# An attention stage with interleaved pieces: the last slot of each step left empty, a wide silu(c), and idle products in bare slots

## The chip, the cores and the metric

The kernel runs on one core of one Trainium2 chip. The time is the device time of one execution in microseconds. Of the kernel before there are three runs: 1338.03, 1338.38 and 1339.69 us, median 1338.38. One more execution was profiled.

## The reference

One transformer block with adaptive layer norm on 8 rows of 512 tokens of width 256 (4096 tokens), all in float32:

```python
mod = (_silu(c) @ wmod).reshape(8, 6, 1, -1)           # c: 8 x 256, wmod: 256 x 1536
sa, ca, ga, sb, cb, gb = (mod[:, k] for k in range(6)) # gates ga, gb: sign kept, size at least 0.25
h = _layernorm(x) * (1 + ca) + sa
x = x + ga * attention(h)     # 16 heads of 16, latent of 64, causal, softmax in full
h = _layernorm(x) * (1 + cb) + sb
x = x + gb * ffn(h)           # 16 experts, each takes its 512 best tokens, and a shared expert
```

In the attention, query and key of a head are `q_lat` (through `q_to_latent`) and `latent_k`, the value is `latent_v`, and `v_up` and `Wout` follow. For the change it matters that the causal logits of a head (512 x 512) are needed twice: once to find each row's maximum, and once, transposed and with the maximum taken off, to be exponentiated and multiplied with the values. Silu(c) is a matrix of 8 x 256 that is multiplied with `wmod` once.

## The kernel before

The kernel has two stages of engine work that follow each other: the attention stage, to about 515 us of the span, and the experts. The change touches only the first.

**Start.** Layer-norm statistics, `sc` = silu(c) transposed (two chunks `k` of 128 partitions x 8, lines 203 to 206), and the products of `sc` with the modulation weights: `pmT` (line 215) gives shift and scale for the first norm; `modulate(n)` (line 227) gives gates and second shift and scale with the 8 columns of `sc` as the stationary operand and 512 columns of weights streaming (`pm`); `modulate_t` (line 234) gives shift and scale of the second norm transposed, with the weights stationary and the 8 columns of `sc` streaming (`pmT2`). `keep_warm` products (line 182) stand at the very start.

**Steps.** Row b and head group g (4 heads) make step n = 4b + g, 32 steps in all. The main loop runs n from -1 to 31. In turn n it works on three steps at once: the contexts (attention times values) of step n-1, `context`, line 678, tile `po`; the transposed scores and exponentials of step n (`scores_t`, tile `st_ps`, and `exps`, line 652); and the plain scores and maxima of step n+1 (`scores`, tile `sc_ps`, and `maxima`, line 627). Contexts stand first, then `fold` (line 640): four transposes of the maxima into `pmx`, and a DVE subtraction from the query strip. After that come six half rounds `k`. A half round takes two heads of the plain scores and two heads of the transposed scores, on different row strips of the array, so that they run side by side, for the tiles that `ROUNDS` names. Within a half round PE gets plain, transposed, plain, transposed; then DVE gets the maxima of the two heads, and ScalarE the two exponentials, with POOL's causal selects behind them.

Plain scores lie in a ring of three PSUM banks (`bank_s`), transposed ones in another (`bank_t`); step -1, which has no transposed scores, uses both. Other products share two banks (`bank`, tag `m`).

**Pieces.** All other products of the attention stage are cut into pieces of about 0.44 us and put between the half rounds: queries (`pq`) and keys (`pk`) of step n+2, transposes (`pt`) and latents (`pl`) of the next row, values (`pv`, line 511), the residual (`py`, line 544), the second norm's transposes and router scores (`pz`, `pzt`), and the shared expert's gate, up and down products (`pg`, `pu`, `py`, lines 303 to 348). `plan(n)` lists a step's pieces, each with an earliest slot, an estimate in us, and DVE work that it brings. There are seven slots: slot 0 ahead of half round 0, and so on to slot 6 behind half round 5, ahead of the next step's contexts. `laid_out` (line 842) places the pieces. It runs a small model of PE and DVE with the constants `ROUND_US`, `HEAD_US`, `CHANGE_US` and `FOLD_US`, gets from it the PE time that each slot should hold (`need`), spreads what is left evenly over the slots, and goes through the pieces in order: each goes into the current slot, or further on if that slot's share is used up. A piece with estimate 0 goes to the slot that the plan names.

Each engine runs its instructions in the order in which this loop issues them. The value piece has a wait of its own: `value(i2, iis)` writes two products into the halves of one PSUM bank, and ScalarE copies each half out after its product:

```python
if ii == 0:
    self.pv = bank("pv").rearrange("p (i h w) -> p i h w", h=H, w=DH)
...
nc.scalar.copy(v[:, i, :, 0:HS:2], self.pv[:, ii, :, :])
```

The second product of a bank waits for the copy of the first. Gate pieces end with a tanh on ScalarE and a DVE product, up pieces with a DVE product (`mid`), residual pieces with a DVE addition. `query` and `key` end with a ScalarE copy and two DMA issues on the SP queue (`spread`, line 581), which bring the rows into the query and key strips.

Of the kernel before, what the change touches and what calls it, by code (L numbers as in the profile page):

```python
# [12 lines left out]
F32 = mybir.dt.float32  # L13
# [8 lines left out]
P = 128  # L22
B, T, D = 8, 512, 256
# [5 lines left out]
KC = D // P  # L29
# [22 lines left out]
def block_kernel(ctx: ExitStack, tc: tile.TileContext, a: dict, out: bass.AP):  # L52
    nc = tc.nc
# [42 lines left out]
    sbT = const.tile([P, KC, B], F32, name="sbT")  # L96
    cbT = const.tile([P, KC, B], F32, name="cbT")
# [18 lines left out]
    ap = att.enter_context(tc.tile_pool(name="att", bufs=2))  # L116
# [13 lines left out]
    wq = wp.tile([P, KC, H * DH], F32, name="wq")  # L130
# [4 lines left out]
    wmod1 = fp.tile([P, 2, KC, 512], F32, name="wmod1", tag="mid")  # L135
# [67 lines left out]
    sc = wp.tile([P, KC, B], F32, name="sc")  # L203
    nc.scalar.activation(sc, cT, AF.Tanh, scale=0.5)
    nc.vector.scalar_tensor_tensor(sc, sc, 1.0, cT, ALU.add, ALU.mult)
    nc.vector.tensor_scalar_mul(sc, sc, 0.5)

    nc.vector.tensor_reduce(strip_one, ident[:, 1::HS], AX.X, ALU.add)

    for t in k_strips:  # L210
        nc.vector.tensor_copy(t, strip_one.to_broadcast([P, T]))
    pmT = bank("pmT")[:, 0 : 2 * KC * B].rearrange("p (m b) -> p m b", b=B)
    for m in range(2 * KC):
        for k in range(KC):
# [11 lines left out]
    mod_sb = wp.tile([B, 4 * D], F32, name="mod_sb")  # L226

    def modulate(n):
        pm = bank("pm")[0:B, :]
        for k in range(KC):  # L230
            nc.tensor.matmul(pm, lhsT=sc[:, k, :], rhs=wmod1[:, n, k, :], start=(k == 0), stop=(k == KC - 1))
        nc.vector.tensor_copy(mod_sb[:, n * 512 : (n + 1) * 512], pm)

    def modulate_t():

        pmT = bank("pmT2")[:, 0 : 2 * KC * B].rearrange("p (m b) -> p m b", b=B)
        for m in range(2 * KC):
            n, c = divmod(m, KC)
            o = (1 - n) * D + c * P
            for k in range(KC):  # L240
                nc.tensor.matmul(
                    pmT[:, m, :],
                    lhsT=wmod1[:, n, k, o : o + P],
                    rhs=sc[:, k, :],
                    start=(k == 0),
                    stop=(k == KC - 1),
                )
        nc.vector.tensor_copy(sbT, pmT[:, 0:KC, :])
        nc.vector.tensor_scalar_add(cbT, pmT[:, KC : 2 * KC, :], 1.0)

    def gate(o):

# [490 lines left out]
    SLOTS = 2 * len(ROUNDS) + 1  # L743

    def plan(n):
# [93 lines left out]
    ROUND_US = (1.04, 1.04, 0.83, 0.83, 0.84, 0.84)  # L839
    HEAD_US = (0.72, 0.72, 0.6, 0.6, 0.78, 0.78)  # L840

    def laid_out(todo):

        slots = [[] for _ in range(SLOTS)]
        extra, given = [0.0] * SLOTS, [0.0] * SLOTS
        for s, us, dve, fn in todo:
            if us == 0.0:
                slots[s].append(fn)
                extra[s] += max(0.0, dve)
                given[s] += max(0.0, -dve)  # L850
        total = sum(us for _, us, _, _ in todo)
        need = [0.0] * SLOTS
        pe = BEGIN_US
        dve = ready = pe + FOLD_US
        for k in range(SLOTS):
            pe += given[k] + (CHANGE_US if k > 0 else 0.0)
            need[k] = max(0.0, ready - pe)
            pe += need[k]
            dve = max(dve + extra[k], pe)
            if k < SLOTS - 1:  # L860
                pe += ROUND_US[k]
                dve = max(dve, pe)
                ready = dve + HEAD_US[k]
                dve += 2 * HEAD_US[k]
        share = min(1.0, total / sum(need))
        rest = max(0.0, total - sum(need)) / SLOTS
        room = [share * sum(need[: k + 1]) + rest * (k + 1) for k in range(SLOTS)]
        done, floor = 0.0, 0
        for s, us, dve, fn in todo:
            if us > 0.0:  # L870
                floor = max(floor, s)
                while floor < SLOTS - 1 and done + us / 2 > room[floor]:
                    floor += 1
                slots[floor].append(fn)
                done += us
        return slots

# [7 lines left out]
    for k in range(2):  # L885
        modulate(k)
# [8 lines left out]
    for n in range(-1, len(steps)):  # L895
        last = steps[n - 1] if n > 0 else None
        now = steps[n] if n >= 0 else None
        nxt = steps[n + 1] if n + 1 < len(steps) else None
        slots = laid_out(plan(n))

        def fill(k):
            for fn in slots[k]:
                fn()

        if last is not None:
            last.context(list(range(TT)))
        if now is not None:
            now.fold()
        fill(0)
        for k in range(2 * len(ROUNDS)):  # L910
            (tiles, cs), half = ROUNDS[k // 2], k % 2

            sc_of, st_of = {}, {}
            at_s = at_t = 0
            for part, (i, c) in enumerate(zip(tiles, cs)):
                for jj in range(2):
                    if nxt is not None:
                        j = 2 * (1 - half) + jj
                        if part == 0:
                            sc_of[j] = bank_t("sc_ps") if nxt.n == 0 and j % 2 else bank_s("sc_ps")  # L920
                        nxt.scores(sc_of[j], j, i, at_s)
                    if now is not None:
                        j = 2 * half + jj
                        if part == 0:
                            st_of[j] = bank_t("st_ps")
                        now.scores_t(st_of[j], j, c, at_t)
                at_s += (i + 1) * P
                at_t += T - c * P
            for jj in range(2):
                if nxt is not None:  # L930
                    j, at = 2 * (1 - half) + jj, at_s

                    for i in reversed(tiles):
# [76 lines left out]
    with tc.tile_pool(name="srch", bufs=2) as sp, tc.tile_pool(name="srch1", bufs=1) as s1:  # L1010
# [22 lines left out]
        for bit in range(29, -1, -1):  # L1033
            part = sp.tile([P, 1], F32, name="part")
# [29 lines left out]
        one = s1.tile([P, 1], F32, name="one")  # L1064
# [27 lines left out]
    with ExitStack() as s:  # L1092
# [219 lines left out]
        for e in range(E):  # L1312
            w, t = weights.pop(e), fetches[e]
# [119 lines left out]
```

## Time and profile before

| what | us |
|---|---|
| runs, median of 3 | 1338.38 (1338.03 to 1339.69) |
| the profiled execution | 1339.74 |
| its span, first to last instruction | 1338.0 |
| TensorE busy in the span | 1306.6 |
| VectorE (DVE) busy | 897.3 |
| GpSimd (POOL) busy | 542.4 |
| ScalarE (ACT) busy | 466.6 |
| mean granted TensorE clock | 0.988 |

Busy time counts the stretches in which an engine has at least one instruction open; for PE, several products can be open side by side. A float32 product of 256 columns shows as two records, x2. In a timeline the columns are start, duration, engine, line, operation, tile written and tiles read, tile shape, operand shape and count; idle time ahead of the group and what ended it stand in brackets. In a table of stretches each engine has its busy time and, in parentheses, its number of instructions; behind them come the granted clock of TensorE as a share of full speed, the busy share of the DMA engines and GB/s.

The fold of each step marks where it begins. Lengths from fold to fold, in us:

| step | from | length |
|---|---|---|
| 0 | 35.40 | 17.06 |
| 1 | 52.45 | 12.34 |
| 3 | 80.32 | 11.36 |
| 6 | 123.06 | 16.54 |
| 8 | 153.39 | 15.42 |
| 13 | 229.78 | 16.36 |
| 14 | 246.14 | 15.43 |
| 24 | 401.56 | 15.96 |
| 28 | 463.56 | 17.82 |

### The profile page before, as it was taken

The page shows a single profiled execution, that of the slowest core. Times are in us where ns is not written, and L with a number is a line of the kernel's source. Part 1 is how long each engine was busy: PE and PEld are TensorE (multiplying, and loading weights), DVE is VectorE, ACT ScalarE, POOL GpSimd, SP SyncE. Part 2 cuts the span into 40 slices and gives each one's busy share as a digit, 9 for nine tenths or more (in the row PEclk, how much of TensorE's full clock was granted, in tenths as well). Part 3 has the DMA queues.
Part 4 walks back from the last instruction along what each step waited for, and adds up shares of the span by engine and source line. Part 5 has one row for each costly group of instructions (what it writes and reads, how often), then busy time and mean ns, then how long its engine had stood idle before and what let it go on. Part 6 is the DMA issues. An engine that isn't in the chain of part 4 may idle for free. (4 is left out here: it accounts for less than half of the span.)

```text
span 1338.0 us, 26423 instructions
## 1 busy us (share of the span) xinstructions
PE 1306.6 (98%) x10286; PEld 929.1 (69%) x10286; DVE 897.3 (67%) x2342; ACT 466.6 (35%) x997; POOL 542.4 (41%) x629
## 2 busy tenths in 40 slices
PE   9999999999999999999999999999999999999996
PEld 5344445445545455877857888888888888888885
DVE  4777676776676765566835777667777677777653
ACT  1455555555555545200112233222233222233221
POOL 4453625253544324010024455534555544555431
PEclk8899999999999999999999999999999999999998
DMA  7112322131313232271024444454444554443511
GB/s 221 60 52 58 86 46 79 40 74 47 85 38 73 57 66 53 38 238 40 21 73 118 114 135 100 128 139 119 110 137 94 138 135 122 108 138 86 145 17 16
DMA packets 84317, 121.93 MB, mean 91 GB/s; under 512 B 14936, under 2 KB 61656, under 8 KB 84192
## 3 DMA queue, kind: packets, MB, share of 16 engines
q1 hardware_dynamic: 69120, 93.76, 23.3%
q0 software_dynamic: 14336, 25.70, 10.2%
q8 instruction: 81, 1.33, 0.4%
q10 hardware_dynamic: 736, 0.79, 0.2%
q14 instruction: 44, 0.36, 0.1%
HBM read 90.33 MB, written 21.51 MB: 84 GB/s over the span
## 5 line engine op out<-in xcount | busy, mean ns | idle before, releaser
L630 DVE CUSTOM_DVE_ANT_0 sc_ps<-sc_ps,causal 128x256 f32<-128x256 f32 (+3 forms) x512 | 245.0, 510 | 89.2 <-PE st_ps L567 73.6
L1261 PE MATMUL epy<-dw,emid 128*128 128x256 f32 x1024 | 236.0, 382 | 1.4 <-ACT xT L1161 0.4
L1286 POOL DMA_INDIRECT out<-eo,idx x64 | 102.0, 1594 | 315.7 <-DVE eo L1278 191.0
L663 ACT ACTIVATE p<-st_ps 128x384 f32<-128x384 f32 (+1 forms) x384 | 181.2, 523 | 137.6 <-PE st_ps L567 135.3
L669 POOL TENSOR_SCALAR_AFFINE_SELECT p<-p 128x256 f32<-128x256 f32 x256 | 104.0, 419 | 286.6 <-ACT p L663 286.5
L1261 PEld LDWEIGHTS epy<-dw,emid 128*128 128x128 f32 x1024 | 192.0, 190 | 37.9 <-DVE emid L1231 12.4
L567 PE MATMUL sc_ps<-k,q 32*64 32x256 f32 (+3 forms) x2048 | 212.8, 458 | 3.6 <-DVE mx L630 3.5
L567 PE MATMUL st_ps<-q,k 32*64 32x128 f32 (+3 forms) x2048 | 209.2, 452 | 0.0
L1208 ACT COPY c<-eu 128x256 f32<-128x256 f32 x120 | 44.7, 373 | 400.3 <-issue 222.8
L1191 PE MATMUL eu<-xsum,wsum 128*128 128x256 f32 x720 | 176.1, 381 | 0.0
L1191 PEld LDWEIGHTS eu<-xsum,wsum 128*128 128x128 f32 x720 | 135.7, 190 | 17.9
L1191 PE MATMUL eu<-xT,gu 128*128 128x256 f32 x480 | 142.8, 379 | 0.0
L567 PEld LDWEIGHTS sc_ps<-k,q 32*64 32x64 f32 x2048 | 78.1, 132 | 79.2 <-issue 39.4
L1210 DVE TENSOR_TENSOR c<-eu,c 128x256 f32<-128x256 f32 x120 | 51.0, 425 | 100.8 <-ACT c L1209 95.5
L1148 POOL DMA_INDIRECT rows<-rows_d,idx x64 | 62.3, 974 | 137.6 <-DVE mid L327 96.4
L1231 DVE SCALAR_TENSOR_TENSOR emid<-eu,ub,esg 128x512 f32<-128x512 f32 x128 | 90.1, 743 | 28.9 <-ACT esg L1227 19.4
L1227 ACT ACTIVATE esg<-eu,gbias 128x512 f32<-128x512 f32 x128 | 81.5, 684 | 58.0 <-PE eu L1191 33.3
L1191 PEld LDWEIGHTS eu<-xT,gu 128*128 128x128 f32 x480 | 91.2, 190 | 12.4
L1211 DVE TENSOR_TENSOR eu<-eu,c 128x512 f32<-128x512 f32 x120 | 83.9, 699 | 4.1
L567 PEld LDWEIGHTS st_ps<-q,k 32*64 32x64 f32 x2048 | 76.8, 131 | 11.1 <-ACT p L663 4.0
L684 PE MATMUL po<-p,v 128*32 128x512 f32 (+3 forms) x1024 | 79.4, 444 | 0.2 <-POOL p L669 0.2
L1108 DVE TENSOR_TENSOR at_q<-pos_lo,iota 128x1024 bf16<-128x1024 f32 x64 | 75.2, 1217 | 0.0
(187 smaller groups left out, 1963.3 us busy)
## 6 DMA issues: line engine op xcount, KB each, us to landing
gu<-in_gw SPq DMA_DIRECT2D x16, 1024.0 KB
gu<-in_up SPq DMA_DIRECT2D x16, 1024.0 KB
dw<-in_dw SPq DMA_DIRECT2D x16, 1024.0 KB
q<-q SPq DMA_DIRECT2D x32, 128.0 KB
rows_d<-mod_d SPq DMA_DIRECT2D x8, 512.0 KB
rows_d<-row SPq DMA_DIRECT2D x8, 512.0 KB
out<-ysb SPq DMA_DIRECT2D x16, 256.0 KB
k<-k SPq DMA_DIRECT2D x30, 128.0 KB
```

The costliest lines, as they stand in the source:

```text
L567: nc.tensor.matmul(out[w : w + P // 2, :], lhsT=lhsT[:, w : w + P // 2], rhs=rhs, start=True, stop=True)
L630: nc.vector.tensor_tensor_reduce(sc_ps[:, at : at + n], sc_ps[:, at : at + n], causal[:, T - n : T], 1.0, -3.0e38, ALU.add, ALU.max, self. ...
L663: nc.scalar.activation(self.all[:, j, :], st_ps[:, 0:n], AF.Exp, scale=SCALE)
L669: nc.gpsimd.affine_select(out=p, in_=p, pattern=[[0, 2], [1, P]], compare_op=ALU.is_ge, fill=0.0, base=0, channel_multiplier=-1,)
L684: nc.tensor.matmul(self.po[self.strip(j), c * P : T], lhsT=v[:, c, self.g * NG + j, :], rhs=self.p[c][:, j, :], start=(c == 0), stop=(c == ...
L1108: nc.vector.tensor_tensor(self.at_q[:, n, :], pos_lo[:, e, n].unsqueeze(2).to_broadcast([P, QT, P]), iota.unsqueeze(1).to_broadcast([P, QT ...
L1191: nc.tensor.matmul(self.u[:, q, :], lhsT=w, rhs=x, start=start, stop=True, skip_group_check=not start)
L1211: nc.vector.tensor_tensor(u[:, 1:3, :], u[:, 1:3, :], c3.unsqueeze(1).to_broadcast([P, 2, HC]), ALU.add)
L1227: nc.scalar.activation(sg, pg, AF.Silu, bias=gbias[:, e, f : f + 1])
L1231: nc.vector.scalar_tensor_tensor(mid[:, f, :], pu, ub[:, e, f : f + 1], sg, ALU.add, ALU.mult)
L1261: nc.tensor.matmul(self.py[:, jj, :], lhsT=self.mid[:, f, j * P : (j + 1) * P], rhs=self.dw[:, f, :], start=(n == 0), stop=(n == NF - 1),)
L1286: nc.gpsimd.indirect_dma_start(out=out[:, :], out_offset=bass.IndirectOffsetOnAxis(ap=t.idx[:, j : j + 1], axis=0), in_=eo[:, jj, :], in_o ...
```

## The change

Four edits are made.

1. `sc_wide` repeats silu(c) sixteen times along the free axis (128 columns per chunk instead of 8), by one POOL instruction. `modulate` takes all 128 columns as the stationary operand and copies out the first 8 rows; `modulate_t` streams 64 columns and copies out the first 8. `pmT` stays as it is.
2. `laid_out` puts no sized piece into slot 6. What is left over is spread over six slots, and the contexts of the next turn follow half round 5 directly. Pieces with estimate 0 that the plan names for slot 6 stay there.
3. `laid_out` notes the load of each slot. In the turns up to n = 5, a half round whose slot holds no sized piece begins with an idle product: a full-array product of 256 columns, written into the first plain-score bank and overwritten by the scores. By the built program there are 3 of them in turn -1, 3 in turn 0, 6 in each of turns 1 and 3, and 1 in turn 4.
4. In half round 0, the plain scores of both heads stand ahead of the transposed ones.

In the built program the pieces of step 8, by slot (0 to 6), stand like this; `pv` is a value, the number is how many:

```
before  pq 3 | pq 1 | pk pv | pk pv | pv | pv pu | pu 3
after   pq 3 | pq 1 | pk pv pk pv | pv 2 | pu 1 | pu 3 | -
```

Steps 12, 16 and 20 are alike. Step 24 has `pv 2` in one slot in both. Step 28 goes from `pk pv | pv 2 pg` to `pk pv 3`.

```diff
+    sc_wide = ap.tile([P, T], F32, name="sc_wide", tag="one", bufs=1)[:, 0 : KC * P]
+    sc_wide = sc_wide.rearrange("p (k r b) -> p k r b", k=KC, b=B)
+    nc.gpsimd.tensor_scalar_mul(sc_wide, sc.unsqueeze(2).to_broadcast([P, KC, P // B, B]), 1.0)
...
     def modulate(n):
-        pm = bank("pm")[0:B, :]
+        pm = bank("pm")
         for k in range(KC):
-            nc.tensor.matmul(pm, lhsT=sc[:, k, :], rhs=wmod1[:, n, k, :], start=(k == 0), stop=(k == KC - 1))
-        nc.vector.tensor_copy(mod_sb[:, n * 512 : (n + 1) * 512], pm)
+            nc.tensor.matmul(
+                pm,
+                lhsT=sc_wide[:, k].rearrange("p r b -> p (r b)"),
...
+        nc.vector.tensor_copy(mod_sb[:, n * 512 : (n + 1) * 512], pm[0:B, :])
...
                     lhsT=wmod1[:, n, k, o : o + P],
-                    rhs=sc[:, k, :],
+                    rhs=sc_wide[:, k, 0 : P // 2 // B, :].rearrange("p r b -> p (r b)"),
...
-            need[k] = max(0.0, ready - pe)
+
+            need[k] = max(0.0, ready - pe) if k < SLOTS - 1 else 0.0
...
-        rest = max(0.0, total - sum(need)) / SLOTS
-        room = [share * sum(need[: k + 1]) + rest * (k + 1) for k in range(SLOTS)]
+        rest = max(0.0, total - sum(need)) / (SLOTS - 1)
+        room = [share * sum(need[: k + 1]) + rest * min(k + 1, SLOTS - 1) for k in range(SLOTS)]
...
-                while floor < SLOTS - 1 and done + us / 2 > room[floor]:
+                while floor < SLOTS - 2 and done + us / 2 > room[floor]:
                     floor += 1
                 slots[floor].append(fn)
+                loads[floor].append(us)
...
+        bare = [n <= 5 and not any(us > 0.0 for us in slot_us) for slot_us in loads]
...
-                for jj in range(2):
-                    if nxt is not None:
+
+                order = [(jj, t) for jj in range(2) for t in range(2)]
+                if k == 0:
+                    order.sort(key=lambda x: x[1])
+                for jj, t in order:
+                    if t == 0 and nxt is not None:
                         j = 2 * (1 - half) + jj
                         if part == 0:
                             sc_of[j] = bank_t("sc_ps") if nxt.n == 0 and j % 2 else bank_s("sc_ps")
+                        if bare[k] and part == 0 and jj == 0:
+
+                            nc.tensor.matmul(
+                                sc_of[j][:, 0 : T // 2], lhsT=wq[:, 0, 0:P], rhs=wq[:, 0, :], start=True, stop=True
+                            )
                         nxt.scores(sc_of[j], j, i, at_s)
-                    if now is not None:
+                    if t == 1 and now is not None:
```

More of the change, by code (lines that the diff above doesn't have):

```diff
@@ L228, in modulate @@
     def modulate(n):
-        pm = bank("pm")[0:B, :]
+        pm = bank("pm")
         for k in range(KC):
-            nc.tensor.matmul(pm, lhsT=sc[:, k, :], rhs=wmod1[:, n, k, :], start=(k == 0), stop=(k == KC - 1))
-        nc.vector.tensor_copy(mod_sb[:, n * 512 : (n + 1) * 512], pm)
+            nc.tensor.matmul(
+                pm,
+                lhsT=sc_wide[:, k].rearrange("p r b -> p (r b)"),
+                rhs=wmod1[:, n, k, :],
+                start=(k == 0),
+                stop=(k == KC - 1),
+            )
+        nc.vector.tensor_copy(mod_sb[:, n * 512 : (n + 1) * 512], pm[0:B, :])
     def modulate_t():
-        pmT = bank("pmT2")[:, 0 : 2 * KC * B].rearrange("p (m b) -> p m b", b=B)
+        pmT = bank("pmT2")[:, 0 : 2 * KC * P // 2].rearrange("p (m b) -> p m b", b=P // 2)
         for m in range(2 * KC):
@@ L247, in modulate_t @@
                 )
-        nc.vector.tensor_copy(sbT, pmT[:, 0:KC, :])
-        nc.vector.tensor_scalar_add(cbT, pmT[:, KC : 2 * KC, :], 1.0)
+        nc.vector.tensor_copy(sbT, pmT[:, 0:KC, 0:B])
+        nc.vector.tensor_scalar_add(cbT, pmT[:, KC : 2 * KC, 0:B], 1.0)
     def gate(o):
@@ L840, in block_kernel @@
     HEAD_US = (0.72, 0.72, 0.6, 0.6, 0.78, 0.78)
+    loads = []
     def laid_out(todo):
         slots = [[] for _ in range(SLOTS)]
+        loads[:] = [[] for _ in range(SLOTS)]
         extra, given = [0.0] * SLOTS, [0.0] * SLOTS
@@ L920, in block_kernel @@
                             sc_of[j] = bank_t("sc_ps") if nxt.n == 0 and j % 2 else bank_s("sc_ps")
+                        if bare[k] and part == 0 and jj == 0:
+                            nc.tensor.matmul(
+                                sc_of[j][:, 0 : T // 2], lhsT=wq[:, 0, 0:P], rhs=wq[:, 0, :], start=True, stop=True
+                            )
                         nxt.scores(sc_of[j], j, i, at_s)
-                    if now is not None:
+                    if t == 1 and now is not None:
                         j = 2 * half + jj
```

## The prediction

> **What bounds the kernel now.** I read the sliced page first, then the clock by stretches, then single steps in order of time.
>
> The page's slices (one digit per 33 us):
>
> ```profile
> PE   9999999999999999999999999999999999999996
> DVE  4777676776676765566835777667777677777653
> PEclk8899999999999999999999999999999999999998
> ```
>
> TensorE has a record open nearly always, so its busy share cannot rank the steps. The attention steps fill the first 16 digits, to about 515 us, and the only low clock digits before the end are the first two. Everything that the diff moves lies there. The next fence gives exact stretches; the columns are the busy time and count of PE, PEld, DVE, ACT and POOL, then the granted clock, DMA share and GB/s.
>
> ```profile
> 19.78:23.19 3.41, 3.41 (x9) 0.63 (x8) 0.68 (x1) 0.59 (x1) 0.00 (x0) 1.00 0.60 132
> 23.19:26.60 3.41, 3.41 (x33) 2.30 (x40) 2.34 (x7) 0.00 (x0) 0.00 (x0) 1.00 1.06 347
> 26.60:33.43 6.83, 6.83 (x62) 3.40 (x47) 4.20 (x17) 0.00 (x0) 0.00 (x0) 0.50 1.10 344
> 33.43:36.84 3.41, 1.94 (x9) 0.91 (x10) 2.67 (x15) 0.59 (x1) 0.00 (x0) 1.00 1.06 369
> 36.84:43.67 6.83, 6.83 (x48) 1.94 (x48) 4.17 (x14) 2.56 (x5) 0.51 (x2) 0.50 0.15 45
> 132.41:135.83 3.42, 2.73 (x46) 1.21 (x38) 2.61 (x14) 3.16 (x8) 0.98 (x3) 1.00 0.58 158
> 135.83:139.24 3.41, 3.41 (x24) 1.09 (x20) 1.40 (x5) 0.89 (x3) 1.22 (x2) 0.50 0.34 77
> ```
>
> The clock is 1.00 or 0.50 for multiples of 3.41 us. Half clock follows 23.2-26.6, 33.4-36.8 and 132.4-135.8. Weighting each product by the share of the array it occupies (a full-array 128x256 record takes 0.21 us from start to start), I estimate that those three stretches use 0.26, 0.31 and 0.29 of the array. The emptiest stretch of the attention steps that was not followed by half clock uses 0.43. So the limit for a drop lies between 0.31 and 0.43. The exception is 19.8-23.2, which is nothing but the eight-column products `pm`: they use 0.06 by columns but 0.99 by rows, and the clock stays. Hence rows that stream seem to count, not columns.
>
> Third, the ends of steps 3 and 14, PE only (start, duration, what):
>
> ```profile
> 89.18 0.27 PE L567 MATMUL st_ps<-q,k 32*64 32x128 f32 x2
> 89.39 2.36 PE L684 MATMUL po<-p,v 128*32 128x512 f32 x32
> 91.68 0.66 PE L645 MATMUL pmx<-ident,mx 128*128 128x128 f32 x4
> ...
> 258.62 0.70 PE L291 MATMUL pu<-h2T,shu 128*128 128x256 f32 x2
> 259.25 2.39 PE L684 MATMUL po<-p,v 128*32 128x512 f32 x32
> 261.57 0.66 PE L645 MATMUL pmx<-ident,mx 128*128 128x128 f32 x4
> ```
>
> In step 3 the contexts already stand directly behind the last half round: 2.29 us later the fold starts, with no wait in the contexts. The last maximum ends at 90.99, 0.69 before it. In step 14 one piece in the last slot adds 0.63.
>
> Fourth, a value pair in one slot, step 24:
>
> ```profile
> 409.45 0.70 PE L516 MATMUL pv<-wlat,lat 64*128 64x256 f32 x2
> 410.79 0.70 PE L516 MATMUL pv<-wlat,lat 64*128 64x256 f32 x2 [0.64 <-ACT v L523]
> ```
>
> The second product waits for ScalarE's copy of the first, which stands behind two exponentials. 1.34 us lie between the starts where 0.53 would do (the key pair at 76.53 to 77.06): 0.81 lost.
>
> **The change, part by part.**
>
> *Wide silu(c).* The new POOL copy queues behind POOL's last setup at 18.54. A tensor-scalar of 128x256 took 1.23 there (`xn`), so it may end at 19.8, as `pm` wants it at 19.77: 0 to 0.2 on the path. `pm` keeps its 512 streamed columns and so its 3.60 us, and by the reading above its clock does not change. `pmT2` streams 64 columns for 8. Its 16 records took 1.95, 0.12 each, which is the pace of weight loads; eight 128-column transposes go at 0.13. So it costs 0 to 0.1, but the use of 23.2-26.6 rises from 0.26 to about 0.5, and the half clock of 26.6-33.4 should go. Step -1 gains little, since its three idle products cost 0.43 + 0.2 each on the same engine and 8.4 us of DVE maxima follow the second pair: -0.3 (from -2 to +1).
>
> *Idle products before step 0 and in it.* Whether 36.8-43.7 gets its clock back depends on the stretch around the fold. There DVE still decides, and I get a use of 0.36 to 0.43, inside the unknown gap. If the clock stays, step 0 (17.06 from fold to fold, 11.3 of DVE) falls to about 14.5, -2.5. If it falls again, the three idle products run at half speed, +1.0. I take -1.2.
>
> *Bare steps 1 and 3*: six idle products each. At 0.43, and 0.2 for changing the tiling, that is 12 x 0.63 = 7.5 if nothing hides it, 0 if DVE does. Step 3 takes 11.36 and DVE works 8.9 of it. The nearest rows are steps with about one piece per slot and a like DVE load, 13.8 to 14.0 (steps 7, 11, 15), which hold 0.5 to 1 more of PE. The first idle product delays DVE's first maximum by 0.5; the third and fourth half rounds have only 1.15 of DVE work to cover 1.45 of PE. I take +1.2 and +1.0: **+2.2**. Steps 2 and 4: a latent product now waits in slot 0 for `hT` (0.43 in other steps), while step 4 loses 1.9 in its last slot: +0.1.
>
> *The last slot.* Where PE is the bound the pieces cost the same elsewhere, and only one change of tiling goes: -0.2 in each of 13 steps (5, 9, 13, 17, 21, 25, 11, 15, 19, 23, 27, 24, 29), **-2.6**. Where DVE is the bound (DVE 12.60 of 15.43 us in step 14) the piece's PE time is hidden in earlier rounds, and 0.63 less 0.1 goes: steps 6, 14, 22, 30, **-2.0**. But what the piece hid comes into view. In step 14 the DVE product for `mid` (0.7) now stands before the last maxima, and the fold's slack was 0.69: 0 lost if it fits, 0.7 if not. I take 0.1, and step 18 at -0.3. Where a gate piece ends in slot 5 (steps 7, 10, 26), the DVE product waits for a tanh that stands behind two exponentials, the last maxima wait behind it, and the fold is about 0.35 late: +0.15 and twice -0.25. SP's queue: the q and k spreads move with their pieces, past the fetch of the inverses; each is needed a step later, so it costs 0.
>
> *Value pairs.* The planner now puts key, value, key, value in one slot and both remaining values in the next, in steps 8, 12, 16 and 20. Behind the waiting product stands PE's whole queue, then DVE's maxima. First pair: the copy ended 1.28 after the product's start in step 8, where 0.55 would do, about 0.79 with the wake-up; second: 0.81. Together 1.6. What of it lasts: steps 20 and 24 hold the same products in as many groups, and the pair makes 15.96 out of 15.42, so 0.54 of 0.81, two thirds. 1.06 less one group at 0.2 is +0.87, four times **+3.5** (bounds 1 and 6.4). Step 28 gets three values in a row, +0.15.
>
> *The clock elsewhere.* In step 6 the contexts start at half clock, and its fold comes 4.70 after the last half round against 3.04 in step 10. Contexts now close up into the empty stretch: -1.7 if the drop goes, I take -1.2. The other way, the stretches with two value waits fall to a use of about 0.37; half a drop at 1.7: +0.8.
>
> **Scores before transposed scores in half round 0** is worth nothing: all eight start within 0.05 us wherever the fold is done (232.38 to 232.41), and in bare steps the idle product fills the wait.
>
> A rule that speaks against the change: the Trainium skill, "TensorE: Matmul & The Clock Gate", section "Why this matters for your kernels", says that only PE-idle gaps above some 3 us bring the clock down. Here the longest idle gap next to a drop is 1.27 us, and PE is recorded busy throughout the first. By the page the idle products buy nothing, nor does the wide operand: -1.5 and -1.2 become about +1.0 and 0, +0.8 goes, and the sum is +1.7. By the trace the drop follows sparse use. I follow the trace.
>
> **Sum:** -0.3 - 1.2 + 2.2 + 0.1 - 2.6 - 2.0 + 0.1 - 0.3 + 0.15 - 0.5 + 3.5 + 0.15 - 1.2 + 0.8 = -1.1. The profiled execution took 1339.74 (span 1338.0, 1.7 around it), so 1338.6 on its footing. The median of the runs is 1338.38, 1.4 less, which gives **1337.3**.
>
> **The rivals.** 0.2%, 2.7 us, is about what a measurement tells from none.
>
> 1. *All of the clock comes back*, and DVE hides more: -2.8 at the start, -1.7 in step 6, no new drop, idle products at +1.5, the last slot at -5.9, values and the rest as above: about -5, 1333.3. For it: the drops stand where the change adds work. Against it: the use around the first fold is at the limit.
> 2. *Slower: the value pairs dig holes for the clock.* In steps 8, 12, 16, 20 the waits last in full (6.4 - 0.8 for the groups, +2.1 over the sum), and three of the stretches between slot 2 and 4 fall under the limit, each with 3.41 us at half clock, 5.1 for the 0.8 taken. That gives -1.1 + 2.1 + 4.3 = +5.3, 1343.7. It decides from a use of about 0.37; step 24, with one wait, is at 0.43 and keeps its clock.
> 3. *The clock doesn't care* (the page's rule): +1.7, 1340.1.
>
> **How the numbers follow.** Forecast 0.38 (its own range 1335.5 to 1340.5, all but 0.04 within 0.2%), rival 1 0.28, rival 2 0.26, rival 3 0.08, half of it slower. Faster 0.28, same 0.40, slower 0.32. The range 1332.5 to 1344.5 takes in both outer rivals and cuts what lies beyond.
>
> **What would show it.** Clock 1.00 from 26.6 on; step 0 near 14.5; steps 1 and 3 at 13.3 and 12.6; contexts 0.1 behind the last half round; `pv` waiting for ACT twice in each of steps 8, 12, 16 and 20, their length near 16.3; no half clock near 136. Half clock anywhere in those four steps, or again behind the first fold, would make the forecast wrong on the slow side; steps 1 and 3 unchanged, on the fast side.

## The result, and the profile after

The changed kernel takes 1350.56 us (median of 6 runs, 1349.05 to 1351.23) against 1338.42 for the kernel before (6 runs, 1336.34 to 1339.69): a ratio of 1.0085, 95% interval 1.0074 to 1.0096. It is slower by about 12 us, beyond the predicted range, on the side of rival 2 and further out than that. The profiled execution took 1350.66, with a span of 1348.9 against 1338.0.

The page's slices of the changed kernel, one digit per 34 us:

```profile
PE   9999999999999999999999999999999999999996
DVE  4767676766676765656744767667777677777653
PEclk9999999999999999999999999999999999999998
```

The two low clock digits at the start are gone, and the mean granted clock rose from 0.988 to 0.991. So the loss is not mainly one of clock: TensorE still has a record open nearly always, and a number of steps take longer. The stretches show where half clock now stands (length; busy time and count of PE, PEld, DVE, ACT, POOL; granted clock, DMA share, GB/s):

```profile
33.95:37.36 3.41, 1.99 (x23) 1.23 (x22) 2.46 (x14) 0.58 (x1) 0.00 (x0) 1.00 1.06 369
37.36:40.78 3.42, 3.42 (x22) 1.08 (x20) 2.14 (x6) 0.78 (x2) 0.00 (x0) 0.50 0.25 79
...
160.24:163.66 3.42, 2.67 (x24) 0.94 (x21) 2.40 (x11) 2.59 (x7) 3.40 (x5) 1.00 0.64 143
163.66:170.48 6.82, 6.67 (x55) 3.37 (x56) 2.97 (x14) 2.23 (x6) 2.79 (x5) 0.50 0.49 115
```

The half clock of 26.6 and that of 135.8 in step 6 have gone, and that behind the first fold has shrunk from two windows to one. A new one of 6.82 us lies in step 8, right behind the stretch into which most of the two waits of its value products fall. Here are its two pairs of value products, PE only, in order of time:

```profile
159.64 0.48 PE L526 MATMUL pv<-wlat,lat 64*128 64x256 f32 x1
159.96 0.38 PE L526 MATMUL pv<-wlat,lat 64*128 64x256 f32 x1
...
160.95 0.70 PE L526 MATMUL pv<-wlat,lat 64*128 64x256 f32 x2 [0.19 <-ACT v L533]
...
162.41 0.70 PE L526 MATMUL pv<-wlat,lat 64*128 64x256 f32 x2
163.81 0.79 PE L526 MATMUL pv<-wlat,lat 64*128 64x256 f32 x1 [0.70 <-ACT v L533]
```

From the first to the second product of a bank it is 1.31 us and then 1.40; both second products wait for ScalarE's copy (L533). The same two waits stand in steps 12, 16 and 20. Before the change the four products of these steps lay in four slots, some 1.5 us apart, and none waited for a copy.

The ends of steps 3 and 14, which the prediction showed of the kernel before, PE only:

```profile
92.62 0.28 PE L577 MATMUL st_ps<-q,k 32*64 32x128 f32 x2
92.83 2.36 PE L694 MATMUL po<-p,v 128*32 128x512 f32 x32
95.12 0.55 PE L655 MATMUL pmx<-ident,mx 128*128 128x128 f32 x3
...
264.75 0.38 PE L577 MATMUL st_ps<-q,k 32*64 32x128 f32 x4
265.06 2.63 PE L694 MATMUL po<-p,v 128*32 128x512 f32 x32
267.63 0.66 PE L655 MATMUL pmx<-ident,mx 128*128 128x128 f32 x4
```

The contexts stand directly behind the last half round, as meant. But in step 14 they take 2.57 us to the fold, where before it was 2.32 (259.25 to 261.57), and step 3 has 2.29. Summed over all steps, PE's busy time in the contexts rose from 79.4 to 84.4. The groups of the changed kernel (busy time, mean ns of one, idle time ahead and what ended it):

```profile
L694 PE MATMUL po<-p,v 128*32 128x256 f32 (+3 forms) x1024 | 84.4, 437 | 2.2 <-POOL p L679 1.9
L526 PE MATMUL pv<-wlat,lat 64*128 64x256 f32 x64 | 23.2, 444 | 7.5 <-ACT v L533 5.4 <-ACT k L595 1.5 <-ACT q L595 0.5
```

and of the kernel before:

```profile
L684 PE MATMUL po<-p,v 128*32 128x512 f32 (+3 forms) x1024 | 79.4, 444 | 0.2 <-POOL p L669 0.2
L516 PE MATMUL pv<-wlat,lat 64*128 64x256 f32 x64 | 22.8, 437 | 1.8 <-ACT v L523 1.8
```

The contexts wait for POOL's causal selects `p`, and the values for ScalarE. Both waits are larger than before, and the values now also wait for copies of `k` and `q`.

Step lengths from fold to fold in the two profiled executions, set beside the steps of the sum:

| steps | predicted | measured |
|---|---|---|
| -1 and 0 | -0.3, -1.2 | +0.73, -1.01 |
| 1 and 3 (idle products) | +2.2 | +0.99 and +1.61 |
| 2 and 4 | +0.1 | +1.12 and -0.40 |
| 5, 9, 13, 17, 21, 25, 29, 11, 15, 19, 23, 27 | -0.2 each, -2.4 | -0.30 in each of the first six, -0.06, then +0.25, +0.40, +0.05, +0.42, -0.29: -1.0 |
| 6, 14, 22, 30 with the clock of step 6 | -3.1 | -1.41, -0.49, -0.10, +0.39: -1.6 |
| 18; 7, 10, 26 | -0.3; -0.35 | +0.53; +0.1 |
| 8, 12, 16, 20 with the clock there | +4.3 | +4.21, +1.26, +1.26, +1.26: +8.0 |
| 24, 28 | -0.2, +0.15 | +1.16, +0.47 |
| from the last fold to the end | 0 | +0.24 |
| sum | -1.1 | +10.9 |

The sum missed by 12.0: 5.4 in the steps with value products (3.7 in steps 8, 12, 16 and 20, 1.7 in 24 and 28), 4.2 at the ends of steps, 2.2 in the first six steps, 0.2 behind.

### The profile page after: what moved, and what is told of

Same layout as the page of the kernel before. It is cut to its first block, busy times and chain, and to the rows that moved or that the text cites. A ratio compares the mean times of both kernels' runs of the same rounds, so it can differ in the third digit from the quotient of the medians.

```text
span 1348.9 us, 26488 instructions
## 1 busy us (share of the span) xinstructions
PE 1312.7 (97%) x10324; PEld 934.8 (69%) x10324; DVE 895.6 (66%) x2342; ACT 467.2 (35%) x997; POOL 542.7 (40%) x630
## 5 line engine op out<-in xcount | busy, mean ns | idle before, releaser
L577 PE MATMUL st_ps<-q,k 32*64 32x128 f32 (+3 forms) x2048 | 204.1, 452 | 0.0
L577 PE MATMUL sc_ps<-k,q 32*64 32x128 f32 (+3 forms) x2048 | 202.5, 452 | 0.2
L577 PEld LDWEIGHTS sc_ps<-k,q 32*64 32x64 f32 x2048 | 73.2, 131 | 72.7 <-issue 38.2
L694 PE MATMUL po<-p,v 128*32 128x256 f32 (+3 forms) x1024 | 84.4, 437 | 2.2 <-POOL p L679 1.9
L577 PEld LDWEIGHTS st_ps<-q,k 32*64 32x64 f32 x2048 | 73.2, 131 | 5.0 <-issue 2.4
```

The costliest lines, as they stand in the source:

```text
L577: nc.tensor.matmul(out[w : w + P // 2, :], lhsT=lhsT[:, w : w + P // 2], rhs=rhs, start=True, stop=True)
L694: nc.tensor.matmul(self.po[self.strip(j), c * P : T], lhsT=v[:, c, self.g * NG + j, :], rhs=self.p[c][:, j, :], start=(c == 0), stop=(c == ...
```

## The experiments

All ratios are against runs of the kernel before on the same chip, with their 95% intervals; us are medians.

| kernel | us | before | ratio |
|---|---|---|---|
| last slot only, on before | 1349.82 | 1339.98 | 1.0079 (1.0050 to 1.0107) |
| changed, last slot open | 1340.25 | 1339.98 | 1.0004 (0.9996 to 1.0013) |
| changed, joint copy | 1336.95 | 1339.98 | 0.9979 (0.9968 to 0.9990) |
| before, joint copy | 1336.20 | 1339.98 | 0.9980 (0.9972 to 0.9989) |
| changed, no idle products | 1348.92 | 1339.02 | 1.0074 (1.0054 to 1.0093) |
| wide silu(c) only, on before | 1338.07 | 1339.02 | 0.9994 (0.9987 to 1.0002) |
| joint copy, idle products in turns -1 and 0 | 1332.23 | 1339.02 | 0.9940 (0.9922 to 0.9957) |
| joint copy, selects of half round 5 left out | 1329.85 | 1339.02 | 0.9920 (0.9901 to 0.9939) |
| joint, idle in -1 and 0, slot closed in some turns | 1329.57 | 1339.87 | 0.9930 (0.9916 to 0.9945) |
| joint, idle in -1 and 0, selects by head | 1335.69 | 1339.87 | 0.9975 (0.9968 to 0.9982) |
| the last two together | 1331.44 | 1339.87 | 0.9939 (0.9924 to 0.9953) |
| joint, idle in -1 and 0, no POOL addition | 1332.49 | 1340.57 | 0.9936 (0.9920 to 0.9953) |

My theory after the result was that the closed last slot alone makes the loss, by moving the value products into pairs that wait. The rivals were the idle products, the clock at the start, and a wait that merely moves to another place.

**1. The four edits taken apart: the last slot alone, and everything but it.**

```diff
-            need[k] = max(0.0, ready - pe)
+            need[k] = max(0.0, ready - pe) if k < SLOTS - 1 else 0.0
...
-                while floor < SLOTS - 1 and done + us / 2 > room[floor]:
+                while floor < SLOTS - 2 and done + us / 2 > room[floor]:
```

(with `rest` and `room` to match), put alone into the kernel before:

> The kernel before, with the planner's rule alone: no sized piece in slot 6. No wide operand, no idle products, the old order in half round 0. Theory A: it holds the whole loss from step 5 on, +9.2 of the 10.7 that the profiles differ by at the last fold, since the pieces stand exactly as in the changed kernel there, but without the idle products' 2.6 in steps 1 and 3: 1346 to 1348, with step 8 at 16.7 or, if the clock falls again, 19.6. Theory C (the loss comes from the idle products and the wide operand, by what they shift): about 1339, no loss in steps 8 to 28.

and the changed kernel with these lines as they were before:

> The changed kernel, with slot 6 open to sized pieces again: the wide operand, the idle products and the order in half round 0 stay. Theory A: steps 5 to 30 as in the kernel before; steps 1 and 3 at 13.3 and 13.0 (+1.0 and +1.6); the start gains or loses within 1.5: 1339.5 to 1342. Theory C: most of the 12 stays, above 1346.

The slot alone gives 1.0079, the other three edits together 1.0004 with 1 inside the interval: without the closed slot no loss is shown. In the profiles, steps 4 to 30 are 6.9 us longer in sum with the slot alone and 7.2 in the changed kernel, but only 0.4 with the slot open, so the loss of these steps is the closed slot's. That the medians agree so well is in part chance. In the profile of the slot alone another 4.5 stand in steps -1 and 0, at half clock (see experiment 3), while the changed kernel pays 2.6 for the idle products of steps 1 and 3. In the profile of the slot alone the half clock falls into another of the four value steps, step 20; the stretches, in the columns of above:

```profile
353.13:356.54 3.41, 2.64 (x24) 0.90 (x21) 2.39 (x11) 2.58 (x7) 3.37 (x5) 1.00 0.65 144
356.54:363.37 6.83, 6.70 (x55) 3.38 (x56) 2.98 (x14) 2.20 (x6) 2.79 (x5) 0.50 0.42 130
```

Its stretch before the drop answers number for number to that of step 8 above (24 matmuls, 11 of DVE, 7 of ACT): the same products. That the clock drops where they happen to fill one 3.41 us window, in step 8 there and in step 20 here, is argued from these stretches.

**2. The waits of the value pairs taken away: one ScalarE copy for both halves of a bank.**

```diff
-                nc.scalar.copy(v[:, i, :, 0:HS:2], self.pv[:, ii, :, :])
+                if ii == 1:
+                    nc.scalar.copy(v[:, i - 1 : i + 1, :, 0:HS:2], self.pv)
```

In the changed kernel:

> The changed kernel, with one edit: ScalarE copies both halves of a value bank out in one instruction after the second product, so that the second product has no copy to wait for. Everything else stays, the pieces' places too. Theory A (the value pairs are the loss: two waits of PE in each of steps 8, 12, 16, 20, one of the two in step 24, one in step 28, and the half-clock stretch that follows the waits in step 8): step 8 falls from 19.63 to 15.4, steps 12, 16 and 20 from 16.68 to 15.2 to 15.4, the clock stays at 1.00 from 44 us to 515 us, and the time falls from 1350.6 by 4.2 + 3 x 1.3 + 0.8 + 0.5 = 9.4 to about 1341. Step 24 keeps its first wait, which is for a bank that the query's copy holds. Theory B (PE would wait there anyway, for DVE or for the exponentials, since the closed-up steps lack cover; the pairs only show where): the waits reappear in the score rounds, the four steps stay above 16, and the time stays above 1347.

and in the kernel before:

> The kernel before, with the one edit of the joint copy. Its adjacent value pairs stand in steps 4, 24 and 28 alone, with 0.68, 0.81 and 0.81 us of wait. Theory A: two thirds of that goes, 1.5 us: 1336.9. If a wait on the copy costs PE nothing in the end (theory B), 1338.4. A loss could come from the first value's copy being late for the contexts, which nothing in the trace suggests.

In the changed kernel the ratio falls from 1.0085 to 0.9979, some 1.05% or 14 us, where 9.4 was expected. The pair no longer waits; the second one of step 8 is now one group of four records:

```profile
158.50 1.13 PE L526 MATMUL pv<-wlat,lat 64*128 64x256 f32 x4
```

Steps 8, 12, 16 and 20 take 14.83 each, against 16.68 with the waits (step 12) and 15.42 before. So the two waits cost 1.85 per step, and the closed slot was worth -0.59 there. No half clock is left in these steps. In the kernel before, the same edit brings 0.2% (steps 4, 24 and 28 fall by 0.8 to 0.9), so about 0.85%, 11 us, is the price of the pairs that the closed slot makes.

The clock's part can be read across the profiles. Closed slot with separate copies: half clock in step 8 (changed), 20 (slot alone) and 28 (without idle products), once in each of the three. In the eleven other profiles there is none between step 7 and the end of the attention steps. In steps 8 and 20 the drop lasts 6.8 us and lengthens the step from 16.68 to 19.6, by 3; in step 28 it lasts 3.4 and costs 1.6 (19.90 against 18.28). The rest of the pairs' price is waiting.

Steps 24 and 28 became longer too, by 1.16 and 0.47, but not by their pairs, which stood there before. With the joint copy in both kernels, step 24 takes 15.06 with the slot open and 16.22 with it closed, and step 28 takes 16.90 and 17.54. In step 24 of the kernel before, the first key product and the first value product start side by side, at 406.39 and 406.40, well behind the last query product. The closed slot puts both directly behind that query product, and the value waits until ScalarE has copied the query. In the changed kernel:

```profile
414.40 0.70 PE L621 MATMUL pk<-lat,wlat 64*128 64x256 f32 x2
415.65 0.70 PE L526 MATMUL pv<-wlat,lat 64*128 64x256 f32 x2 [0.55 <-ACT q L595]
```

In step 28 a value now waits 0.82 for the copy of a key. Both waits stand in the joint copy's profile as well; no run took them away.

**3. The idle products.** All left out of the changed kernel (`bare` never true), and, on the joint copy, kept in turns -1 and 0 only (`n <= 5` becomes `n <= 0`):

> The changed kernel without its 19 idle products; wide silu(c), order and the closed last slot stay. Cost theory: the idle products of turns 1 and 3 lengthened steps 1 and 3 by 0.99 and 1.61 and those come back, -2.6; the ones in turns -1 and 0 had bought at most the 1.0 of step 0, so about 1349, steps 1 and 3 at 12.34 and 11.36. Clock theory: the idle products are what holds the clock at the first fold; without them half clock stands behind 23.2-26.6 or the first fold for two windows or more, step 0 goes to 17 or above, and the time is 1350.5 or above in spite of the -2.6.

> The changed kernel with one ScalarE copy for both halves of a value bank, and idle products only in turns -1 and 0. Additive theory: the 1336.95 of the joint copy less the 0.99 + 1.61 of steps 1 and 3 is 1334.3. Rival: the idle products of steps 1 and 3 hold the clock there; without them a window at half clock falls into steps 1 to 4 and the time is 1337 or above.

Without any, the time is 1.0074, which is not told apart from 1.0085. Steps 1 and 3 do fall back (12.07 and 11.73), and the start pays for it: in that profile the clock stays at half from 33.6 for 20.5 us and step 0 takes 22.00. With those of turns -1 and 0 kept and the others gone the ratio is 0.9940 against 0.9979. Steps 1 and 3 are 2.7 shorter (12.08 and 11.49), as expected; the 5 us of the medians are more than that, and where the rest comes from stays open, as the start differs from execution to execution. Steps -1 and 0 together take 51.5 on average in the nine profiles with idle products there (49.9 to 54.6) and 53.6 in the five without (50.3 to 56.9). These five show what the idle products are needed for: with the slot open step 0 takes 17.05 or 17.06 in all three, with it closed 21.41 and 22.00, with 17 and 20 us at half clock around the first fold in place of 6.8. The runs say the same: those of the two closed kernels without idle products are spread over 13.2 and 11.1 us, the slowest at a mean clock of 0.981 or 0.982, the fastest at 0.993.

**4. The wide silu(c) alone.**

> The kernel before with the wide silu(c) alone. Reading of the prediction: the array is fuller in 23.2-26.6, the half clock of 26.6-33.4 goes, step -1 gains 0.3 (at most 1), the rest stays: 1338.1. Rival (the clock heeds only idle gaps of the engine): half clock at 26.6 stays, 1338.4. Second rival: without idle products the half clock comes one window later, over the maxima, and nothing is won: 1338.4 with half clock between 30 and 44.

Its stretches at the start, in the columns of above:

```profile
23.19:26.60 3.41, 3.41 (x40) 2.28 (x44) 2.35 (x7) 0.00 (x0) 0.00 (x0) 1.00 1.09 355
26.60:30.99 4.39, 4.39 (x63) 2.46 (x47) 3.79 (x15) 0.00 (x0) 0.00 (x0) 1.00 1.09 347
30.99:34.41 3.42, 1.55 (x9) 0.79 (x9) 2.68 (x15) 0.58 (x1) 0.00 (x0) 1.00 1.09 350
34.41:41.23 6.82, 6.82 (x48) 1.89 (x50) 4.16 (x12) 2.43 (x5) 0.41 (x1) 0.50 0.45 148
```

The half clock at 26.6 goes, though PE shows as busy there as before. The other profiles agree: in the three without the wide operand half clock begins between 26.6 and 28.9, in none of the eleven with it. The edit widens the products `pm` and `pmT2` together, and no run widened one alone. Step -1 is 2.1 shorter in this profile (0.3 was forecast, at most 2), step 0 the same. In the medians no difference is shown: 0.9994, with 1 inside the interval. The rule of idle gaps of the engine, rival 3, foresaw no change of the clock here.

**5. What the contexts wait for.** With the joint copy, the causal selects of half round 5 are left out, so the last two heads of the last tile pair go into the contexts unmasked:

```diff
-                if j % 2 == 0:
+                if j % 2 == 0 or (j == NG - 1 and cs == ROUNDS[-1][1]):
                     continue
```

> The changed kernel with the joint copy, and with the causal selects of half round 5 (the last two heads of the last tile pair) left out in every step: 64 POOL instructions less, the contexts read those probabilities unmasked. Theory: with the last slot closed the contexts wait for these selects, 0.3 to 0.6 in steps 2, 6, 10, 18, 19, 22, 26, 30 and 0.25 to 0.4 in steps 11, 15, 23, about 4 in all, which comes back: 1333, those steps 0.3 to 0.6 shorter. Rival: the exponentials or the last maxima end as late as the selects, and the wait only changes its name: 1336 to 1337, steps unchanged within 0.15.

0.9920 against 0.9979, and steps 4 to 30 are 7.9 shorter in sum, twice what was expected. Steps 6, 18, 19, 22 and 30 fall by 0.7 to 1.0, 2, 7, 15 and 23 by 0.43 to 0.55, the others by 0.35 or less: the contexts do wait for these selects. What delays the selects was the next question. By head instead of by tile, so that only one select of two stands behind the last exponential:

```diff
+            if len(cs) == 2:
+                p = self.all[:, j, :].rearrange("p (c w) -> p c w", w=P)[:, 0:3:2, :]
+                nc.gpsimd.affine_select(
+                    out=p,
+                    in_=p,
+                    pattern=[[0, 2], [1, P]],
...
+                return
```

> The joint copy, idle products only in turns -1 and 0, the last slot closed everywhere; in the last two half rounds the causal selects go by head (each both tiles of one head, behind that head's exponential) in place of by tile (each both heads, behind both exponentials). As many selects of the same size, nothing left out. Theory: with one select instead of two behind the last exponential the contexts' wait is about half gone, and so is half of what leaving the selects out brought (7 in all): 1328.7. Rival: the selects wait for POOL or for the port and not for the exponentials, and nothing moves: 1332.

It became slower: 0.9975, and steps 15, 18, 19 and 23, among others, lose 0.34 to 0.42 each. In the profiles steps 4 to 30 lose 2.3 in sum, half of what the medians say; the rest stays open. My theory of the exponentials fell. POOL's own queue at the end of step 18 shows why. The timeline of POOL alone, first in the kernel before:

```profile
321.34 1.30 POOL L669 TENSOR_SCALAR_AFFINE_SELECT p<-p 128x256 f32<-128x256 f32 x2 [0.90 <-ACT p L663]
323.06 1.27 POOL L357 TENSOR_TENSOR ysb<-ysb,x_all 128x512 f32<-128x512 f32 x1 [0.42 <-DVE ysb L353]
```

The same in the changed kernel:

```profile
328.69 1.28 POOL L367 TENSOR_TENSOR ysb<-ysb,x_all 128x512 f32<-128x512 f32 x1 [0.25 <-DVE ysb L363]
329.93 1.21 POOL L679 TENSOR_SCALAR_AFFINE_SELECT p<-p 128x256 f32<-128x256 f32 x2
```

And with the selects by head:

```profile
315.58 1.28 POOL L367 TENSOR_TENSOR ysb<-ysb,x_all 128x512 f32<-128x512 f32 x1 [0.63 <-DVE ysb L363]
316.82 1.21 POOL L677 TENSOR_SCALAR_AFFINE_SELECT p<-p 128x256 f32<-128x256 f32 x2
```

The residual piece used to be in the last slot, and POOL's addition came behind the selects. The closed slot moves the piece one slot ahead, and its 1.28 us of POOL work stand ahead of the selects, which then start behind it without a wait. By head, both selects still start there, but the contexts of the third tile now need both instead of one. So the addition was left out (those rows go out without `x`):

```diff
-            eng.tensor_tensor(ysb, ysb, x_all[:, n : n + 2, :], ALU.add)
+            if not self.early:
+                eng.tensor_tensor(ysb, ysb, x_all[:, n : n + 2, :], ALU.add)
```

> The joint copy, idle products only in turns -1 and 0, the last slot closed everywhere, and POOL's addition of x to the shared expert's residual (4 instructions of 1.28 in the attention stage, at the ends of steps 18, 19, 29 and 30) left out: those rows go out without x. Theory (the selects stand behind other POOL work that the closed slot has moved ahead of the last half round): steps 18, 19 and 30 fall by 0.6 to 1.0 each, steps 15, 22 and 23, where no addition stands, stay within 0.1; about 1330. Rival (the selects wait for the exponentials, or are only slow beside DVE's product for the contexts): steps 18, 19 and 30 stay within 0.2 of 16.75, 16.80 and 15.38, 1332.

POOL at the end of step 18 without the addition:

```profile
315.29 0.77 POOL L681 TENSOR_SCALAR_AFFINE_SELECT p<-p 128x256 f32<-128x256 f32 x2 [1.75 <-ACT p L675]
316.96 0.77 POOL L681 TENSOR_SCALAR_AFFINE_SELECT p<-p 128x256 f32<-128x256 f32 x2 [0.91 <-ACT p L675]
```

Steps 18 and 19 fall from 16.75 and 16.80 to 15.81 each, 30 by 0.37 (0.6 to 1.0 expected), 29 by 0.21; 15, 22 and 23 stay within 0.02. The selects wait for the exponentials again, and the pair takes 0.77 instead of 1.21, since it is all but over when DVE's product for the contexts' heads starts. The steps' sum is 2.5 us; the medians (0.9936 against 0.9940) do not resolve it.

This gives back more than the move had cost. In step 19 the addition stood ahead of the selects in the kernel before too, and the change made that step only 0.05 longer, step 18 0.53. In step 30 the addition alone costs nothing: in the profiles of the slot alone and without idle products it stands ahead, both selects take 0.41, and the step takes 14.91 and 14.92. It is 15.34 to 15.38 only where DVE's product also slows a select.

In steps 14 and 22 no addition stands, and the profiles show the cause. Seven kernels have the slot closed there and keep the selects. In eight of their fourteen steps one select takes 0.86 or 0.87 beside DVE's product, and the step takes 15.33 or 15.34; in the other six both selects take 0.41, and it takes 14.94 to 14.96. Here is the pair in step 22, first in the changed kernel, then with the joint copy and idle products in turns -1 and 0:

```profile
394.79 1.23 POOL L679 TENSOR_SCALAR_AFFINE_SELECT p<-p 128x256 f32<-128x256 f32 x2 [0.91 <-ACT p L673]
...
381.94 0.77 POOL L680 TENSOR_SCALAR_AFFINE_SELECT p<-p 128x256 f32<-128x256 f32 x2 [0.91 <-ACT p L674]
```

With the slot open the same difference is worth 0.04 at most (15.39 to 15.43).

In steps 15 and 23 it is POOL's whole queue. Before and after, POOL goes from its second select of the step to its last without a pause of more than 0.11 us, for 8.1 us, with the products of the routed row between the selects, and the fold comes 0.47 behind the last select. So these steps are as late as that second select. In step 15, before and after:

```profile
267.04 0.41 POOL L669 TENSOR_SCALAR_AFFINE_SELECT p<-p 128x256 f32<-128x256 f32 x1 [1.14 <-ACT p L663]
...
273.52 0.41 POOL L679 TENSOR_SCALAR_AFFINE_SELECT p<-p 128x256 f32<-128x256 f32 x1 [1.52 <-ACT p L673]
```

From the step's fold it is 5.47 to this select before (fold at 261.57) and 5.89 after (267.63). The closed slot has put a second gate piece ahead of the half round whose exponential it waits for. The step became 0.40 longer. With the slot open again (experiment 6) the select is back at 5.46.

**6. A version made from this:** joint copy, idle products in turns -1 and 0, and the slot closed only in turns with n mod 4 of 0 or 1 and in turn 6; then with the selects by head too.

```diff
-        slots = laid_out(plan(n))
+        slots = laid_out(plan(n), 1 if n % 4 < 2 or n == 6 else 0)
```

> The joint copy, idle products only in turns -1 and 0, and the last slot closed only where it paid: in turns with n mod 4 of 0 or 1 and in turn 6; elsewhere it is open as before. Additive theory: steps 18, 15, 23, 30, 27, 11 win back 0.53, 0.42, 0.43, 0.37, 0.48, 0.27, steps 14 and 22 give up what the closed slot won them (0.1 to 0.4 each): about -2 against the same kernel with the slot closed everywhere (1332.2), 1330. Rival: that kernel's waits for the selects were hidden by something else, and the time stays 1332 to 1333.

> Both at once: selects by head, and the last slot closed only in turns with n mod 4 of 0 or 1 and in turn 6, on the joint copy and the idle products of turns -1 and 0. If the two edits cure the same wait they do not add: about 1328.5, the better of the two less at most 1. If they add, 1326.5.

The first takes 1329.57, 0.9930 (0.9916 to 0.9945), and is the fastest here that leaves nothing out: 0.7% below the kernel before, and some 1.5% below the changed one. Steps 15, 18, 23 and 30 are back at 14.03, 16.21, 14.10 and 15.00, within 0.1 of before, while the -0.3 of steps 5, 9, 13, 17, 21 and 25 and the 14.83 of the value steps stay. In the steps from 4 on it gains 1.8 on the same kernel with the slot closed everywhere, as expected; the medians (0.9930 and 0.9940) have overlapping intervals. The selects by head add nothing (0.9939).

## Why the prediction was wrong, and where it was right

**The value pairs: the failed step.** The prediction found the pairs and both waits, and sized the waits at 1.6 in sum. The failed working is that "two thirds" of it last, taken from steps 20 and 24 as equal but for one wait. They are not: with the waits gone from the kernel before (joint copy), step 24 takes 15.06 and step 20 15.47. Step 24's wait thus cost 0.90, all of its 0.81, and step 20 was 0.4 too long as a yardstick. In the changed kernel nothing of the waits is hidden: 1.85 per step, less 0.59 for the closed slot, +1.26 for the +0.87 forecast. In steps 24 and 28, put down at -0.2 and +0.15, the prediction followed only the pairs. It missed that a value would come so close behind a query or a key that it waits for ScalarE's copy of that one: +1.16 and +0.47, which the joint copy does not take back. That these waits make up the whole of it is not shown, since no run took them away.

**The clock in the value steps.** The limit was read rightly: rival 2 said that it decides from a use of about 0.37, and by the same estimate the stretch ahead of the drop in step 8 has 0.36. What failed is the size: "half a drop at 1.7" stands against one drop in each of the three profiles, of 3 in two of them and 1.6 in the third. In steps 8 and 20 it lasts two windows, since the next stretch, at half clock, has a use of about 0.31. Rival 2 was the right mechanism, but inherited the other errors of the sum.

**The last slot.** Where PE is the bound and POOL is free, -0.3 came for -0.2 (steps 5 to 25 with n mod 4 = 1). What failed is "0.63 less 0.1 goes: steps 6, 14, 22, 30, -2.0", and with it "what the piece hid comes into view", where only DVE's product and its maxima were followed. POOL's queue was left out, put at nothing without a reason. The contexts now stand directly behind the last half round and have to wait for selects that end later. The profiles show three causes: an addition that moved ahead of the selects with its piece (step 18), a select slowed beside DVE's product (22, and 30 together with the addition), and a POOL queue without a pause that starts later (15 and 23). Steps 15 and 23, listed at -0.2 as bound by PE, were bound by POOL before the change too. Together these five steps are some 3.3 of the 4.2 that the ends of steps missed; the rest is not traced. Step 14 came as forecast, -0.49, but by luck: its selects happened to run clear of DVE's product. The experiment without those selects gives back more, 7.9, so it frees contexts also in steps that had not become longer.

**The start.** Steps 1 and 3 came at 13.33 and 12.97 for the 13.3 and 12.6 that were named. Step 0 at 16.05 lies between the 14.5 of the forecast and 17.06, with half clock again behind the first fold. Step -1 is +0.73 for -0.3. With a spread of some 3.5 us in this step between profiles, one execution cannot settle these sizes. Of step 2's +1.12 the wait for `hT` (0.43) had been named; that its contexts wait for the selects as well had not, and the rest is not traced.

**The clock in step 6** was right: half clock between 132 and 140 is in all four profiles with the last slot open there and in none of the ten with it closed. So was rival 3's rejection: around the new drop in step 8 the longest idle gap of TensorE is 0.70.

## What to carry to other kernels

When work is moved to make a gap on one engine, write out every queue that the moved piece feeds, here POOL's addition, and see what it is now ahead of. Ask also of each step which engine works without a pause up to its end, here POOL in steps 15 and 23, and what starts that work: a piece put ahead of it is paid in full. Two products that share a bank with a copy between them are cheap only while something stands between them: ask for the wait in full unless a row shows work in that place, and take a step as a yardstick only if its time without the wait is known. One copy for both halves removed the wait and made the closed slot useful where POOL was free.

## What the runs showed of the hardware

The granted clock followed how much of the array is used, and with a narrower limit than the prediction had. With the prediction's estimate of array use for each 3.41 us window, over all fourteen profiles from 24 us to the end of the attention steps, windows at full clock that were followed by half clock have 0.26 to 0.38, and those that were not have 0.37 or more, the eight-column `pm` products excepted. Windows at half clock that stayed have 0.38 or less, and those that rose 0.38 or more. So the limit lies near 0.375 in both directions. This is an estimate from the products' sizes, not a counter.

A pair of selects on POOL takes 0.77 by itself and 1.21 to 1.30 where DVE's 128x512 product for the heads falls beside the second, which then goes from 0.41 to 0.85 or more. Over the fourteen profiles all 47 such selects that take over 0.6 (0.73 to 0.96) overlap that product. But 73 others overlap it by over 0.1 us and keep 0.40 to 0.59, and in some of these cases it is the product that is longer, up to 0.94 for 0.69. That the two share something is argued from the rows; no run kept the two apart on purpose.
